# Heads and norm on ScalarE or GpSimd only, and another list of seeds for the order of a transformer block

## The chip, the cores and the metric

The kernel runs on one core of a Trainium2 chip. The metric is the time of one execution on the device in microseconds; the time before is the median of three runs, 952.11 us (951.52 to 952.36). The profile comes from one more execution, recorded by the hardware profiler. In it, TensorE multiplies matrices (PE; its weight loads are shown as PEld), VectorE (DVE), ScalarE (ACT) and GpSimd (POOL) do the element-wise work, and SyncE (SP) issues nearly all transfers. Each engine works through its own instructions strictly in order; semaphores hold an instruction back until what it needs is done.

## What is computed

A post-norm transformer block in float32: attention with grouped heads, then a gated feed-forward layer, each followed by a residual sum and a layer norm. There are 2 batches of 512 tokens, a model width of 512, 32 query heads and 8 key and value heads of width 128, and an inner width of 1376. Cut to what matters here:

```python
q = (x @ Wq.T).reshape(b, s, H, HD).transpose(0, 2, 1, 3)
k = (x @ Wk.T).reshape(b, s, HKV, HD).transpose(0, 2, 1, 3)
v = (x @ Wv.T).reshape(b, s, HKV, HD).transpose(0, 2, 1, 3)
q = _rmsnorm(q, q_norm_w)      # t * rsqrt(mean(t*t) + EPS) * w, over each head
k = _rmsnorm(k, k_norm_w)
scores = jnp.einsum('bkgqd,bksd->bkgqs', qg, k) / math.sqrt(HD)
bias = jnp.where(rel > 0, NEG_INF, slopes[:, :, None, None] * rel)
attn = jax.nn.softmax(scores + bias[None], axis=-1)
out = jnp.einsum('bkgqs,bksd->bkgqd', attn, v)
# ... out @ Wo.T, x = layernorm(x + attention), x = layernorm(x + ffn)
```

The part that the change names is `_rmsnorm`: the heads times their norm.

## The kernel before

**Tiles and stages.** The tokens of a batch are cut into four blocks of 128. A *unit* is (group g, batch b, block i): 8 groups of four query heads with one key and value head, 2 batches, 4 blocks, 64 units. Two neighbouring units make a *pair*, and there are 32 pairs. For each pair, `project` forms q, k and v of two blocks (with seven half-size products in place of eight: `seven`, L747; only the first pair is projected plainly, L867), `heads` normalises and transposes them, `scores` forms the scores and the softmax of each unit, `attend` multiplies with v, and `project_out` or `project_pair` multiply with Wo. After the attention come the layer norm (`norm1`), the feed-forward products (`ffn_up`, `ffn_down`) and the last layer norm.

**The heads and their norm** (`heads`, from L988). For each of the two blocks r of a pair, ScalarE squares 5 heads of 128 columns (four of q, one of k, L1002), VectorE reduces them to `ms` (L1025), GpSimd takes the power -1/2 (`rsqrt`, L674) into `inv`, and then `normed` multiplies the heads by `inv` into `sq`. This last step can be done in two ways: as one product of 128x640 with a broadcast operand on VectorE or GpSimd (L1072), or as five scaled copies of 128x128 on ScalarE (L1065). There are 64 such steps. From `sq`, VectorE transposes into `c` (L1188), which goes through `far_q` in DRAM (L1201) back into `qT` (L1212), and k is weighted into `kT` (L1226, L1228). The first pair goes over TensorE transposes instead (L1145, L1160).

**Scores and attention.** A score matmul (L1263) writes `sc`, VectorE adds the bias and takes the row maximum (L1272), ScalarE takes the exponential (L1288), VectorE the reciprocal of the row sums (L1303), ScalarE or GpSimd scale the rows (L1320, L1322). VectorE transposes squares of 32 into `st` (L968), SyncE stores `st` to `far` in DRAM (L977) and loads it back turned as `prT` (L1385), two loads for each block, and TensorE multiplies it with v (`pa`, L1408). Units 0, 1 and 63 are turned on TensorE instead (`pt`, L1359).

**Transfers.** All on SyncE's queue but for the first loads of xT and the last store, which stand on ScalarE's. Beside `far`, `prT`, `far_q` and `qT` these are the loads of weights: `w` of a group in chunks of 384 KB (L486), `wo` in one load of 1 MB (L541).

**What sets the order.** Every operation is first recorded as an op (`Work.add`): the engines that may do it with an estimated cost for each, a priority, and what it reads and writes. `emit` then plans and issues. `order` is a list scheduler: it keeps the free times of the engines and, step by step, takes the ready op that could start first; among ops of one engine that could start at the same time, the one of lowest `prio` wins. If an op may run on several engines, the engine is chosen there too. The order so found becomes the fixed order of each engine's instructions. Before that, `shift` is called once for every number in `SHIFTS` (L79): it takes the number as a random seed, draws a place in the range of priorities and a reach, and adds random amounts to the priorities of the ops there. The priorities of the plan are thus those written in the code plus the sum of all these shifts.

For the heads, the choice of engine is written so:

```python
NORMED = {"DVE": dve(5 * HD) + 0.2, "POOL": pool_tt(5 * HD), "ACT": 5 * act(HD, True)}
WHO = ("DVE", "POOL", "ACT")
...
W.add({k: NORMED[k] for k in WHO}, prio, normed, ...)
```

Of the kernel before, what the change touches and what calls it, by code (L numbers as in the profile page):

```python
# [60 lines left out]
def act(n, scaled=False):  # L61
    return 0.15 + 0.00084 * n + (0.1 if scaled else 0.0)


def dve(n):
    return 0.15 + 0.00106 * n


def pool_tt(n):
    return 0.27 + 0.00197 * n  # L70


def pool_ts(n):
# [3 lines left out]
LAG = {"PE": 0.22, "DVE": 0.1, "ACT": 0.12, "POOL": 0.2, "SP": 0.1, "ACTQ": 0.1, "NONE": 0.0}  # L77
TABLE = 1.28
SHIFTS = (  # L79
    42000001, 42000003, 42000019, 42000038, 42000046, 42000048, 42000080, 42000095, 42000168,  # L80
    42000176, 42000217, 42000257, 42000262, 42000308, 42000360, 42000448, 42000460, 42000471,
    42000478, 42000488, 42000493, 42000503, 42000508, 42000510, 42000517, 42000520, 42000530,
    42000532, 42000548, 42000582, 42000707, 42000844, 42000865, 42000884, 42000922, 42000957,
    42000970, 42000975, 42001005, 42001037, 42001049, 42001090, 42001148, 42001238, 42001283,
    42001404, 42001444, 42001471, 42001476, 42001778, 42002042, 42002048, 42002090, 42002122,
    42002149, 42002330, 42002340, 42002665, 42002784, 42002821, 42003002, 42003036, 42003133,
    42003139, 42003188, 42003348, 42003694, 42003791, 42004290, 42004466, 42005040, 42005857,
    42006497, 42006735, 42006892, 42007003, 42007117, 42007158, 42007651, 42008481, 42008514,
    42009150, 42011723, 42012356, 42012546, 42013135, 42013648, 42014108, 42014321, 42014614,
    42014976, 42015318, 42015996, 42016788, 42016932, 42017026, 42017104, 42017164, 42020579,  # L90
    42020641, 42021783, 42021971, 42022454, 42022740, 42023193, 42023363, 42024350, 42024865,
    42025415, 42026349,
)
NORMED = {"DVE": dve(5 * HD) + 0.2, "POOL": pool_tt(5 * HD), "ACT": 5 * act(HD, True)}
WHO = ("DVE", "POOL", "ACT")
ALONE = lambda p, r: False


# [255 lines left out]
def post_ln_block(  # L354
# [631 lines left out]
    def heads(p, prio):  # L986
# [67 lines left out]
        for r in range(2):  # L1054


            def normed(e, r=r):
# [16 lines left out]
            W.add(  # L1074
                {k: NORMED[k] for k in WHO},
                prio,
# [1167 lines left out]
```

## Time and profile before

| | |
|---|---|
| runs, median of 3 (lowest, highest) | 952.11 us (951.52, 952.36) |
| the profiled execution, its own time | 954.71 us |
| of it the span, first to last instruction | 952.9 us |
| granted TensorE clock, mean | 0.997 |
| transferred in the span | 157.46 MB, 165 GB/s |
| scores (L1263) on TensorE | 154.1 us in 512 records |
| projections (L747, all forms of `_q`) on TensorE, first form | 90.3 us in 248 records |
| power -1/2 (L674) on GpSimd, mean | 1966 ns |
| heads times norm on ScalarE (L1065) | 165 copies, mean 397 ns |
| landing of a prT load, median | 3.2 us |

How to read it: the profiled execution is one execution, and a little longer than the runs without a profile, so a sum over its instructions is compared with its own time. A float32 matmul gives two records in the trace, so 4254 records of TensorE stand for fewer instructions. Matmuls are pipelined: a record of 486 ns for 384 columns overlaps the next, and what counts is the distance from start to start, 1.29 us for four of them. The 40 slices of the span show TensorE at 9 tenths or more in all but the first and the last, and a granted clock of 9 tenths or more throughout. An idle time of TensorE is shown with what ended it; a wait of another engine costs nothing as long as TensorE doesn't wait in turn.

### The profile page before, as it was taken

The page shows a single profiled execution, that of the slowest core. Times are in us where ns is not written, and L with a number is a line of the kernel's source. Part 1 is how long each engine was busy: PE and PEld are TensorE (multiplying, and loading weights), DVE is VectorE, ACT ScalarE, POOL GpSimd, SP SyncE. Part 2 cuts the span into 40 slices and gives each one's busy share as a digit, 9 for nine tenths or more (in the row PEclk, how much of TensorE's full clock was granted, in tenths as well). Part 3 has the DMA queues.
Part 4 walks back from the last instruction along what each step waited for, and adds up shares of the span by engine and source line. Part 5 has one row for each costly group of instructions (what it writes and reads, how often), then busy time and mean ns, then how long its engine had stood idle before and what let it go on. Part 6 is the DMA issues. An engine that isn't in the chain of part 4 may idle for free.

```text
span 952.9 us, 14098 instructions
## 1 busy us (share of the span) xinstructions
PE 940.2 (99%) x4254; PEld 682.6 (72%) x4254; DVE 713.3 (75%) x1767; ACT 485.2 (51%) x1347; POOL 549.3 (58%) x608
## 2 busy tenths in 40 slices
PE   8999999999999999999999999999999999999997
PEld 5655776766767675767677766676677888888886
DVE  7777877778877878887878888787776766675464
ACT  3676665656565656465746566565652433433100
POOL 5774775657494837775768686866564412232040
PEclk9999999999999999999999999999999999999999
DMA  9269758555583847657678786569852323310011
GB/s 324 67 199 258 232 157 241 170 184 174 176 234 107 267 132 222 206 186 198 172 239 225 235 214 190 174 184 263 217 176 81 86 81 89 85 52 23 1 45 44
DMA packets 196876, 157.46 MB, mean 165 GB/s; under 512 B 28384, under 2 KB 179680, under 8 KB 195520
## 3 DMA queue, kind: packets, MB, share of 16 engines
q1 hardware_dynamic: 195936, 155.90, 54.8%
q8 instruction: 34, 0.56, 0.2%
q10 hardware_dynamic: 864, 0.66, 0.2%
q14 instruction: 42, 0.34, 0.1%
HBM read 97.60 MB, written 58.46 MB: 164 GB/s over the span
## 4 chain that ended last, share of the span: by engine, by line
PE 96%; DMA 2%; SPq 1%; DVE 0%; issue 0%; POOLq 0%; DVEq 0%
PE pa_q L747 17%; PE sc L1263 13%; PE pa L1408 12%; PE pb_q L747 8%; PE pa_h L747 8%; PE pa_o L1632 8%; PE pb_h L747 4%; PE pc_q L747 4%; PE pb_o L1632 4%; PE pa_d L747 4%; PE pa_o L747 3%; PE pc_o L1632 2%; PE pc_h L747 2%; PE pb_d L747 2%; PE px L1440 2%; DMA prT<-far 2%
## 5 line engine op out<-in xcount | busy, mean ns | idle before, releaser
L1288 ACT ACTIVATE pr<-pr,nmax 128x48 f32<-128x48 f32 (+15 forms) x256 | 133.4, 522 | 91.2 <-DVE nmax L1272 90.1
L1263 PE MATMUL sc<-kT,qT 128*128 128x512 f32 (+15 forms) x512 | 154.1, 409 | 0.0
L1272 DVE CUSTOM_DVE_ANT_0 pr<-sc,bias 128x48 f32<-128x48 f32 (+15 forms) x256 | 109.7, 442 | 34.3 <-PE sc L1263 31.5
L1408 PE MATMUL pa<-prT,v 128*128 128x512 f32 (+1 forms) x306 | 129.6, 512 | 2.7 <-DMA prT<-far 2.7
L1263 PEld LDWEIGHTS sc<-kT,qT 128*128 128x128 f32 x512 | 88.2, 191 | 48.2 <-issue 21.9
L1320 ACT ACTIVATE pr<-pr,rden 128x64 f32<-128x64 f32 (+12 forms) x221 | 95.4, 495 | 23.1 <-DVE rden L1303 22.8
L688 DVE TENSOR_TENSOR acc<-acc,pa_o 128x512 f32<-128x512 f32 (+2 forms) x128 | 72.7, 568 | 44.9 <-PE pa_o L1632 28.2
L968 DVE STREAM_TRANSPOSE st<-pr 128x512 f32<-128x512 f32 (+1 forms) x153 | 92.1, 634 | 1.6 <-ACT pr L1320 0.6
L747 PE MATMUL pa_q<-tq,sx 128*128 128x384 f32 x248 | 90.3, 487 | 0.0
L1408 PEld LDWEIGHTS pa<-prT,v 128*128 128x128 f32 x306 | 54.0, 191 | 24.3 <-issue 6.4
L674 POOL TENSOR_TENSOR inv<-ms,nhalf 128x10 f32<-128x10 f32 (+1 forms) x33 | 64.9, 1966 | 7.8 <-DVE ms L1039 5.4
L848 ACT COPY gu<-pa_h 128x256 f32<-128x256 f32 (+1 forms) x88 | 31.8, 370 | 73.3 <-PE pa_h L747 62.7
L1002 ACT ACTIVATE sq<-c 128x640 f32<-128x640 f32 x64 | 45.7, 730 | 38.3 <-DVE c L1188 32.9
L747 PEld LDWEIGHTS pa_q<-tq,sx 128*128 128x128 f32 x248 | 45.5, 190 | 26.9 <-issue 5.5
L848 ACT COPY c<-pa_q 128x384 f32<-128x384 f32 x73 | 34.5, 473 | 54.2 <-PE pa_q L747 47.4
L1065 ACT ACTIVATE sq<-c,inv 128x128 f32<-128x128 f32 x165 | 51.9, 397 | 15.0 <-POOL inv L674 15.0
L1188 DVE STREAM_TRANSPOSE c<-sq 128x320 f32<-128x320 f32 x124 | 55.8, 485 | 0.0
L1025 DVE TENSOR_REDUCE ms<-sq 128x5 f32<-128x640 f32 x64 | 51.4, 810 | 1.2 <-ACT sq L1002 1.2
L1632 PEld LDWEIGHTS pa_o<-ti,si 128*128 128x128 f32 x336 | 43.1, 192 | 7.2 <-issue 3.6
L688 POOL TENSOR_TENSOR so<-aT,aT 128x512 f32<-128x512 f32 x23 | 29.3, 1274 | 32.8 <-PE pa_o L1632 31.7
L1322 POOL TENSOR_SCALAR pr<-pr,rden 128x64 f32<-128x64 f32 (+7 forms) x67 | 31.1, 473 | 29.4 <-DVE rden L1303 28.3
L1288 ACT ACTIVATION_READ_ACCUMULATOR pr<-pr,nmax 128x1 f32 x256 | 48.0, 188 | 0.0
(245 smaller groups left out, 2216.9 us busy)
## 6 DMA issues: line engine op xcount, KB each, us to landing
far<-st SPq DMA_DIRECT2D x122, 256.0 KB, 3.1
prT<-far SPq DMA_DIRECT2D x244, 128.0 KB, 3.2
far_q<-c SPq DMA_DIRECT2D x31, 640.0 KB, 3.9
qT<-far_q SPq DMA_DIRECT2D x62, 320.0 KB, 3.8
w<-in_wqkv_dram SPq DMA_DIRECT2D x39, 384.0 KB, 4.6
wo<-in_wot_dram SPq DMA_DIRECT2D x10, 1024.0 KB, 5.8
far<-st SPq DMA_DIRECT2D x31, 128.0 KB, 2.7
prT<-far SPq DMA_DIRECT2D x62, 64.0 KB, 3.0
```

The costliest lines, as they stand in the source:

```text
L674: lambda e: nc.gpsimd.tensor_tensor(dst(), src(), nhalf[:, :n], ALU.pow),
L688: lambda e: vec[e].tensor_tensor(dst(), a(), b(), alu),
L747: nc.tensor.matmul(bank[:rows, :width], lhsT=a(fa, c), rhs=b(fb, c), start=(fresh and c == 0), stop=(c == depth - 1), skip_group_check=True,)
L848: nc.scalar.copy(dst(), src())
L968: {"DVE": dve(n)}, prio, lambda e: nc.vector.transpose(dst(), src()), reads, [A(st)]
L1188: lambda e, r=r, m=m: nc.vector.transpose(cb[:, m] .rearrange("p n w -> p (n w)")[:, :half] .rearrange("p (m r h d) -> p r h m d", m=2, r= ...
L1263: lambda e, a=a, w=w, sc=sc: nc.tensor.matmul(sc[:, :w], lhsT=qT[:, r, a, : G * Q], rhs=kT[:, :w], start=True, stop=True),
L1272: lambda e, a=a, w=w, sc=sc: nc.vector.tensor_tensor_reduce(out=pr[:, a, :w], in0=sc[:, :w], in1=bias[:, S - w :], scale=-(SHRINK**-g), sc ...
L1288: lambda e, a=a, w=w: nc.scalar.activation(pr[:, a, :w], pr[:, a, :w], AF.Exp, bias=nmax[:, a : a + 1], scale=-1.0, accum_out=den[:, a : a ...
L1320: nc.scalar.activation(dst, src, AF.Copy, scale=rden[:, a : a + 1])
L1408: lambda e, j=j, prT=prT, n=n: nc.tensor.matmul(by_head(po.tile)[:, :, P - n // G :], lhsT=v[:, j, :], rhs=late(prT, j, n), start=(j == 0) ...
L1632: nc.tensor.matmul(bank[:, ts(c, P)], lhsT=a(fa, c), rhs=b(fb, c), start=fresh and c == 0, stop=True, skip_group_check=True,)
```

## The change

It does two things. `WHO` no longer names VectorE, so that the planner can give the product of heads and norm to GpSimd or ScalarE alone. And the list of 110 seeds is replaced by another of 102, sought among 72000 numbers; not one is kept. Both go into the planner, which orders all ops anew: the operations, their sizes and their costs are the same, but for the engine of those that may run on several. The diff, cut in the middle of the two lists:

```diff
 TABLE = 1.28
 SHIFTS = (
-    42000001, 42000003, 42000019, 42000038, 42000046, 42000048, 42000080, 42000095, 42000168,
...
-    42025415, 42026349,
+    122000003, 122000005, 122000008, 122000019, 122000028, 122000065, 122000089, 122000102,
...
+    122065376, 122065661, 122065761, 122066904, 122067471, 122071425,
 )
 NORMED = {"DVE": dve(5 * HD) + 0.2, "POOL": pool_tt(5 * HD), "ACT": 5 * act(HD, True)}
-WHO = ("DVE", "POOL", "ACT")
+WHO = ("POOL", "ACT")
 ALONE = lambda p, r: False
```

## The prediction

> **What bounds the kernel now.** I read the busy shares first, then the chain of waits, then TensorE's own waits, because an engine at 99% can still hide slack.
>
> ```profile
> PE 940.2 (99%) x4254; PEld 682.6 (72%) x4254; DVE 713.3 (75%) x1767; ACT 485.2 (51%) x1347; POOL 549.3 (58%) x608
> ...
> PE 96%; DMA 2%; SPq 1%; DVE 0%; issue 0%; POOLq 0%; DVEq 0%
> ```
>
> TensorE is the bound: busy 940.2 of 952.9 us, and 96% of the chain that ended last. VectorE is in the chain with 0%, so an instruction taken from it is worth nothing by itself. What can be gained is what TensorE waits for, by the view of waits with TensorE alone:
>
> ```profile
> PE pa L1408 <- DMA prT<-far: 2.7, 2, 2.1
> PE pp L867 <- DMA w<-in_wqkv_dram: 1.8, 1, 1.8
> PE warm L554 <- POOL ident masks.py:199: 1.3, 1, 1.3
> PE pb_q L747 <- DVE ms L1039: 0.5, 1, 0.5
> PE pp L867 <- DMA xT<-in_xt_dram: 0.4, 1, 0.4
> ```
>
> Where they lie is in the timeline of TensorE. The first is the wait at the head, the next two lie around 688 us:
>
> ```profile
> 9.87 7.98 PE L867 MATMUL pp<-w,xT 128*128 128x384 f32 x24 [1.77 <-DMA w<-in_wqkv_dram]
> ```
>
> ```profile
> 685.65 0.33 PE L1263 MATMUL sc<-kT,qT 128*128 128x64 f32 x2
> 688.09 2.05 PE L1408 MATMUL pa<-prT,v 128*128 128x512 f32 x2 [2.11 <-DMA prT<-far]
> 689.92 0.61 PE L1263 MATMUL sc<-kT,qT 128*128 128x112 f32 x2
> 690.33 1.58 PE L747 MATMUL pa_o<-to,so 128*128 128x256 f32 x4
> 691.75 1.02 PE L1408 MATMUL pa<-prT,v 128*128 128x512 f32 x2
> ```
>
> The stall costs more than its 2.11 us. A pair of 128x512 products takes 0.86 us from start to start elsewhere in the chain; here it takes 689.92 - 688.09 = 1.83. The pair of 112 columns takes 0.41 where it takes 0.22, the four of 256 take 1.42 where they take 0.86, and the start is 2.22 late: 2.22 + 0.97 + 0.19 + 0.56 = 3.9 us. The table by stretches (columns: sum of the stretch, busy time of the five engines, granted clock, DMA share, GB/s) says why:
>
> ```profile
> 688.00:690.00 2.00, 1.92 (x3) 0.92 (x4) 0.00 (x0) 0.74 (x3) 0.37 (x1) 0.50 0.98 321
> 690.00:692.00 2.00, 2.00 (x8) 1.71 (x7) 0.34 (x3) 0.48 (x2) 0.00 (x0) 0.65 0.20 68
> ```
>
> The granted clock is 0.50 and 0.65 there. **Rule against row:** the Trainium skill, "TensorE: Matmul & The Clock Gate" (What's actually happening), has the array fall to half rate after an idle window of about 3.4 us. The idle row here is 2.11 us and the clock fell all the same, so the measurement decides: a stall of this size is priced at 3.9 us; by the rule it would be 2.2.
>
> **What the change does, part by part.** The work is the same: the built orders of both kernels hold 2170 TensorE and 682 SyncE instructions. What moves is the order, on every engine.
>
> *The norm's engine.* Of the 64 products of heads and norm, 7 stood on VectorE, 24 on GpSimd, 33 on ScalarE; now it is 0, 31, 33. The rows by line:
>
> ```profile
> L1072 POOL TENSOR_TENSOR sq<-c,inv x24: 1250/1256/1346, 49.4 to 666.1; 128x640 f32<-128x640 f32 x24
> ...
> L1072 DVE TENSOR_TENSOR sq<-c,inv x7: 817/820/2434, 38.9 to 523.5; 128x640 f32<-128x640 f32 x7
> ```
>
> VectorE gives up 7 x 1.10 = 7.7 us (mean 1101 ns), GpSimd takes 7 x 1.26 = 8.8. The skill speaks against this: "GPSIMD Engine Reference" (Engine selection) sends elementwise work to VectorE and calls GpSimd about twice as slow for two inputs. By that rule each move costs its chain some 1.1 us, by the medians 0.44, by the means, with the one 2434 ns instruction, 0.16. I take 0.44. It lies beside other work: from a pair's last product to its first score matmul the new order leaves at least 20.2 us of TensorE work (22.7 before). The chain between them by rows: 0.56 sum, 0.74 squares, 0.81 reduce, 0.2, 1.98 power, 1.26 norm, 4 x 0.45 transposes, 3.9 landing, 0.55 issue, 3.8 landing, 0.4 weighting = 16.0. That covers 0.44 nine times, so the move costs 0; without the cover, 7 x 0.44 = 3.1. Nor is VectorE relieved: counted by kind, with mean durations from the rows, other two-input sums move to it, and its total goes up by 4.8 us, GpSimd's goes down by 14.5, ScalarE's by 4.4. All stay under TensorE.
>
> *The head.* The chain from the start runs through SyncE's issues of qw and kw (0.43 us each), then the last chunk of w, issued at 5.47 and landed at 9.73. The new order issues that chunk before qw and kw: 0.95 us earlier (5.47 - 4.52), so about 8.8. More: TensorE now takes the chunks of w in the order in which they are issued, so ten products, not four, stand ahead of the first that needs the last chunk. The first four end at 5.04 + 3.06 = 8.10; six more of 0.645 us put the demand at 11.97. The wait of 1.77 us goes: -0.95 at least, -1.77 taken. Late next is the second half of xT of batch 1: it lands up to 9.5 us after an issue at 8.51, at 18.0, and is wanted at 8.10 + 7.74 + 3 x 1.29 = 19.7. I take 0, up to +1.
>
> *At 20.93* TensorE waits 0.51 us behind VectorE's sum on xT; the new order has that sum on GpSimd, several instructions ahead. -0.5 (ends 0 and -0.7).
>
> *At about 40 us* the second unit gets tight: 0.43 us of TensorE work between its last transposes and the product that reads their eviction, where an eviction of 128x512 by ScalarE takes 0.59. With hand-overs: +0.4 (0 to 1).
>
> *The two stalls on prT.* Both waits (648.10, 0.61 us idle and slower after it, 0.8 in all; and 688.09) are for loads of prT that SyncE issues right behind a 1 MB load of wo: 7.5 and 7.0 us in the chain, where the page's median to landing is 3.2. As a measure I take the TensorE work, from rows, between the last TensorE event that the load's issue depends on through deps, buffers and queue order, and the matmul that reads it. Behind a load of wo this lead was 8.6 at the first stall and 9.8 at the second; 7.9 and 10.5 to 10.9 at others that did not stall. At the same two loads of wo the new order has 23.6 and 11.3. I take both stalls as gone: -0.8 and -3.9 (ends: both stay, 0); late next there is the next block of prT, with over 10.
>
> *What comes instead.* The trace cannot show the new order, so bounds. A plain chain to prT costs by rows 0.44 (scores on VectorE) + 0.63 (transposes) + 0.36 (issue of far) + 2 x 0.57 (issues of prT) + 3.2 (landing) = 5.8 us. The new order's tightest leads of several steps are 5.6 (with four issues of prT: 2.3 + 3.2 = 5.5), 6.9, 7.3, 7.4, 7.6 and 7.7 (with three transposes: 7.0); before they were 6.6, 7.0, 7.1, 7.3. Behind loads of wo it has 7.9 and 8.3, behind loads of w 7.5 and 7.9, where 7.7 did not stall before. So nothing must stall, and more places can. Below: 0. Above: two stalls like that at 688, 7.8. I take 2.5, nearest to one short stall and its slow clock.
>
> **Sum**, against the profiled execution (954.71 us, of it span 952.9): -1.8 - 0.5 + 0.4 - 0.8 - 3.9 + 2.5 = -4.1, so 950.6. That execution lies 2.6 above the median of the runs, 952.11; the same difference gives **948.0**.
>
> **Rivals.** *Slower: stalls behind weights.* One mechanism: SyncE's queue is in order, and a load of w waits there for TensorE to release its buffer; the prT loads queue behind it and share the DMA engines with it. Places: w of group 3 ahead of the first unit of group 1 (lead 7.5), wo of groups 1 and 3 (8.3, 7.9), w of group 6 (7.9). For it: in both stalls before, landing took over 7 us. Against: leads of 7.7 and 7.9 held. Each costs 3.9 us; without new stalls the sum is -6.6, so two bring +1.2, and it decides from the third: 952.1 - 6.6 + 11.7 = 957.2. *Same: the gain is eaten.* One stall like that at 688, and only 0.95 won at the head: -5.8 + 3.9 = -1.9, 950.2, and with xT late, 951.5. *The words only:* engine shares move, TensorE's waits don't: 952.1, since no VectorE time is on the chain. Against it: the head's issue order is different in the built program.
>
> **Numbers.** A measurement of this kernel tells 0.2% or 1.9 us from no change. Forecast, 948.0 (944.8 to 950.2): 0.73. Gain eaten, 951.5: 0.12. Words only, 952.1: 0.04. Slower, 957.2 (and milder, from 954.0): 0.11. Faster 0.73, same 0.16, slower 0.11. The range goes from 944.8 (no new stall, -6.6, and the ends of the small terms) to 952.8, which takes in both middle cases and leaves the slow one out.
>
> **What would show it.** Right: the second batch of pp starts near 8.1, not 9.87; no wait of TensorE on prT near 648 and 688; clock 1.00 in all stretches between; VectorE busy near 718, GpSimd near 535. Wrong: waits of TensorE on prT of over 2 us, with a load of w or wo issued just ahead; or a wait on xT at 20 us that gives the head back.

## The result, and the profile after

The change makes the kernel slower: 957.48 us, median of 4 runs (956.76 to 957.96), beside 952.24 (951.52 to 953.07) for the kernel before. The ratio is 1.0051 with a 95% interval of 1.0039 to 1.0064; the forecast was 948.0 with a range to 952.8. In the experiments below the kernel before was run again with each set, 951.3 to 956.1 with medians of 952.7 to 953.2.

The page of after, busy times and the chain that ended last:

```profile
span 956.2 us, 14134 instructions
...
PE 941.0 (98%) x4254; PEld 681.6 (71%) x4254; DVE 715.5 (75%) x1782; ACT 481.4 (50%) x1336; POOL 536.9 (56%) x604
...
PE 92%; DMA 5%; DVE 1%; SPq 1%; ACT 0%; issue 0%; POOL 0%; POOLq 0%; DVEq 0%; ACTq 0%
```

TensorE is still the bound, and its own work is the same. Its share of the chain is down from 96% to 92%, and DMA is up from 2% to 5%: what was added is waiting. The view of TensorE's waits (total us, times, longest us):

```profile
PE pa L1408 <- DMA prT<-far: 5.4, 6, 1.4
PE pb_q L747 <- POOL xT L688: 1.7, 1, 1.7
PE warm L554 <- POOL ident masks.py:199: 1.3, 1, 1.3
```

The head did what was forecast: all 32 records of `pp` stand in one row of the timeline, without a wait, and `pa_q` follows at 15.72, where it stood at 17.68 before.

```profile
4.38 11.50 PE L867 MATMUL pp<-w,xT 128*128 128x384 f32 x32
15.72 1.45 PE L747 MATMUL pa_q<-w,xT 128*128 128x384 f32 x4
```

The waits at 20.93, 648 and 688 are gone too. In their place, the timeline of TensorE in after:

```profile
45.48 1.56 PE L747 MATMUL pb_q<-w,xT 128*128 128x384 f32 x4 [1.72 <-POOL xT L688]
...
690.53 1.13 PE L1408 MATMUL pa<-prT,v 128*128 128x512 f32 x2 [1.18 <-DMA prT<-far]
...
694.04 1.10 PE L1408 MATMUL pa<-prT,v 128*128 128x512 f32 x2 [1.09 <-DMA prT<-far]
...
702.72 1.10 PE L1408 MATMUL pa<-prT,v 128*128 128x512 f32 x2 [0.70 <-DMA prT<-far]
...
711.97 1.10 PE L1408 MATMUL pa<-prT,v 128*128 128x512 f32 x2 [1.41 <-DMA prT<-far]
```

One long stall has become many short ones: one near 45 us, four within 22 us at the end of the attention, and three of 0.3 to 0.55 at 81.7, 460.6 and 555.3, which other executions of this order of TensorE have in part or not at all.

To see where the time went, I subtract TensorE's own work from its clock. Each product is counted at its undisturbed distance from start to start (1.29 us for four records of 384 columns, others in proportion; a record of fewer than 128 columns counts as 128, and a group of the `px` and `pz` products as the 1.08 that it takes); the sum up to a given product is its position. Time of the trace less position is what TensorE has lost by then. The marks are the groups of `px` products (L1440), sixteen in each kernel, of which the first, the thirteenth and the last are taken. All values in us, of one profiled execution each:

| kernel | lost up to the first mark | first to thirteenth | thirteenth to last | sum |
|---|---|---|---|---|
| before | 7.2 | 7.3 | 6.1 | 20.7 |
| after | 7.9 | 8.9 | 7.1 | 23.9 |

(Before: marks at 88.99, 624.79, 731.19, positions 81.8, 610.2, 710.5. After: 86.61, 623.18, 736.93, positions 78.7, 606.4, 713.1.) The difference of 3.2 is nearly all of the 3.3 between the spans. The head's gain of 2 is used up by the first mark, 1.6 is lost in the middle, and the last stretch, whose two stalls went, loses 1.0 more than before. The 1.6 is the least firm of these: among the executions below, the middle loses 7.3 to 8.0 in the order of before and 7.4 to 9.8 in the order of after, though none of their moves but that of the norms lies in it. By kind, the 3.2 are 3.9 more at the starts that a wait delayed (9.6 against 5.7 over their undisturbed distance), 1.4 less of slow clock (0.5 against 1.9, 1.7 of it behind the stall at 688), and 0.7 in the small rest. The runs differ by 5.2, not 3.3; why is taken up with the second group of experiments.

### The profile page after: what moved, and what is told of

Its sections match the earlier page's. It is cut to its first block, busy times and chain, and to the rows that moved or that the text cites. A ratio compares the mean times of both kernels' runs of the same rounds, so it can differ in the third digit from the quotient of the medians.

```text
span 956.2 us, 14134 instructions
## 1 busy us (share of the span) xinstructions
PE 941.0 (98%) x4254; PEld 681.6 (71%) x4254; DVE 715.5 (75%) x1782; ACT 481.4 (50%) x1336; POOL 536.9 (56%) x604
## 4 chain that ended last, share of the span: by engine, by line
PE 92%; DMA 5%; DVE 1%; SPq 1%; ACT 0%; issue 0%; POOL 0%; POOLq 0%; DVEq 0%; ACTq 0%
PE pa_q L747 16%; PE sc L1263 12%; PE pa L1408 10%; PE pa_h L747 8%; PE pa_o L1632 8%; PE pb_q L747 8%; PE pb_h L747 4%; PE pb_o L1632 4%; PE pc_q L747 4%; PE pa_d L747 4%; DMA prT<-far 2%; PE pa_o L747 2%; DMA qT<-far_q 2%; PE pc_o L1632 2%; PE pc_h L747 2%; PE pb_d L747 2%
## 5 line engine op out<-in xcount | busy, mean ns | idle before, releaser
L1263 PE MATMUL sc<-kT,qT 128*128 128x240 f32 (+15 forms) x512 | 152.8, 408 | 0.6 <-ACT kT L1226 0.3
L1320 ACT ACTIVATE pr<-pr,rden 128x64 f32<-128x64 f32 (+12 forms) x210 | 90.6, 495 | 18.8 <-DVE rden L1303 18.6
L848 ACT COPY c<-pa_q 128x384 f32<-128x384 f32 x80 | 37.8, 474 | 76.6 <-PE pa_q L747 72.3
L1322 POOL TENSOR_SCALAR pr<-pr,rden 128x64 f32<-128x64 f32 (+12 forms) x78 | 37.1, 485 | 50.0 <-DVE rden L1303 49.6
L747 PE MATMUL pb_q<-w,xT 128*128 128x384 f32 x124 | 45.5, 489 | 1.7 <-POOL xT L688 1.7
```

Source lines behind the costliest of these rows:

```text
L747: nc.tensor.matmul(bank[:rows, :width], lhsT=a(fa, c), rhs=b(fb, c), start=(fresh and c == 0), stop=(c == depth - 1), skip_group_check=True,)
L848: nc.scalar.copy(dst(), src())
L1263: lambda e, a=a, w=w, sc=sc: nc.tensor.matmul(sc[:, :w], lhsT=qT[:, r, a, : G * Q], rhs=kT[:, :w], start=True, stop=True),
L1320: nc.scalar.activation(dst, src, AF.Copy, scale=rden[:, a : a + 1])
```

## Experiments

Four kernels change the engine or the plan; the others leave the plan as it is and move single ops in the finished order, with a helper put into `emit` (`move(ns, to)` puts the ops with these numbers, one by one, ahead of op `to`). TensorE's order is untouched by these moves, so the marks can be compared between kernels. The inserted lines shift the line numbers in their profiles by 4 to 11.

```diff
-        for o in self.order():
+        placed = self.order()
+        def move(ns, to):
+            for n in ns:
+                o = next(x for x in placed if x["n"] == n)
+                placed.remove(o)
+                placed.insert(next(i for i, x in enumerate(placed) if x["n"] == to), o)
+        ...
+        for o in placed:
```

| kernel | median, us | ratio to before | 95% interval |
|---|---|---|---|
| after | 957.48 | 1.0051 | 1.0039 to 1.0064 |
| norm_to_gpsimd | 952.78 | 0.9996 | 0.9987 to 1.0005 |
| norm_to_vectore | 959.02 | 1.0063 | 1.0051 to 1.0076 |
| engines_alone | 969.39 | 1.0169 | 1.0152 to 1.0185 |
| seeds_alone | 981.51 | 1.0303 | 1.0288 to 1.0318 |
| before_head | 951.78 | 0.9988 | 0.9980 to 0.9996 |
| before_wo | 950.59 | 0.9977 | 0.9965 to 0.9989 |
| before_both | 949.90 | 0.9973 | 0.9962 to 0.9983 |
| before_three | 950.08 | 0.9966 | 0.9953 to 0.9978 |
| xT_first | 956.72 | 1.0036 | 1.0024 to 1.0049 |
| vn_later | 954.52 | 1.0009 | 1.0001 to 1.0018 |
| wo_later | 958.10 | 1.0055 | 1.0040 to 1.0070 |
| three_moves | 959.49 | 1.0064 | 1.0052 to 1.0076 |
| after_mended | 959.92 | 1.0078 | 1.0065 to 1.0092 |
| after_two | 954.20 | 1.0014 | 1.0007 to 1.0020 |
| after_four | 954.68 | 1.0017 | 1.0010 to 1.0025 |

### Is it the engine?

**norm_to_gpsimd**: the order of before, and only the engine of seven ops changed.

```diff
+        for o in placed:
+            if o["fn"].__name__ == "normed" and o["eng"] == "DVE":
+                o["eng"] = "POOL"
```

> The order of before, kept as it is, with only the 7 products of heads and norm that stood on VectorE given to GpSimd. Theory (the order costs the time, not the engine): no change, 952.2, at most +1. Rival (the engine costs it: each of the 7 norms is later and its pair's scores with it): +3 to +5, 955 to 957.

**norm_to_vectore**: the order of after, and the same seven pairs back on VectorE (`c_1`, `c_8`, `c_10`, `c_13`, `c_16`, `c_21`, `c_24`).

> The order of after, kept as it is, with the products of heads and norm of the same 7 pairs given from GpSimd to VectorE. Theory (order): no change against after, 957.5, within 1. Rival (engine): 3 to 5 less, 953 to 954.5.

Moving the seven norms to GpSimd costs nothing: 0.9996, with both ends within 0.13%. Its profile has all of them on GpSimd (this view gives the shortest, median and longest duration in ns), VectorE 6.5 us less busy and GpSimd 9.1 more than before:

```profile
L1076 POOL TENSOR_TENSOR sq<-c,inv x31: 1255/1257/1481, 38.4 to 665.8; 128x640 f32<-128x640 f32 x31
```

```profile
PE 939.0 (99%) x4254; PEld 681.4 (72%) x4254; DVE 706.8 (74%) x1760; ACT 484.9 (51%) x1347; POOL 558.4 (59%) x615
```

The way back gains nothing either (1.0063 beside 1.0051, the intervals overlap). The rival is out: the engine of the norm, by itself, is not where the 5 us come from.

**engines_alone** and **seeds_alone**: one half of the diff each, planned anew.

> The kernel before with WHO of two engines and the old seeds, planned anew. Theory (order): a third order with waits of its own; its time can be on either side, 948 to 960, and its distance from before equals the difference of TensorE's waits and slow rows. If it is slower than before while the first kernel of this set is not, the planner's order and not the engine did it. Rival (engine): 955 to 957, with waits of TensorE on kT or qT behind the power and the norm.

> The kernel after with WHO of three engines again, and the new seeds, planned anew. Theory (order): a fourth order, 948 to 960; sums over TensorE's waits explain it. Rival (engine): the time of before or less, 952 or below, since VectorE may take norms again.

Both missed the range given: 969.39 and 981.51. Each half alone is far worse than both together, so the effects of engine list and seeds don't add. In seeds_alone one wait for VectorE is of 5.8 us, the longest in any of these kernels:

```profile
PE sc L1263 <- DVE nmax L1272: 6.0, 2, 5.8
```

Neither list of seeds did well with the other choice of engines, and a small difference in the plan's input gave an order with other waits. Before and after are both orders with few waits, and what tells them apart is a handful of places.

### What were the gains worth?

**before_head** takes over the head's order of loads in part, **before_wo** moves the two loads of `wo` that stood ahead of the stalled loads of `prT`, **before_both** does both.

```diff
+        move([7], 11)            # before_head, before_both: chunk of w
+        move([3361], 3554)       # before_wo, before_both: wo of group 7, batch 0
+        move([3643], 4023)       # before_wo, before_both: wo of group 6, batch 1
```

> Before, with one load moved on SyncE: the chunk of w that TensorE wants for its fifth product goes ahead of two chunks that it wants later, and of qw and kw. Theory (the head's gain of the new order is this load's place): the wait of 1.77 at 9.87 goes, -1.8 against before, 950.9. Rival (the start is bound by what lands behind it, xT or the other chunks): no change, 952.8.

> Before, with two loads of wo (1 MB) moved on SyncE: that of group 7, batch 0, behind the two prT loads that it delayed at 648, that of group 6, batch 1, behind the four that it delayed at 688. Theory (as the prediction had it, both stalls are loads of prT behind a load of wo and go with it): -4.7 against before, 948. Rival (the 1 MB takes its time on the DMA engines wherever it stands, and the next loads of prT, with leads no longer, stall in their place): -1 to +2, 952 to 955.

> Before, with the moves of both. Theory: their sum, -6.5, 946.3. Rival: -1.8 to 0, 951 to 953.

Every gain has the sign foreseen, and every one is smaller: 1.2 per mille at the head (1.1 us) instead of 1.8 us, 2.3 per mille for the two stalls (2.2 us) instead of 4.7, and 2.7 per mille (2.6 us) for both. The two waits on `prT` are gone. TensorE's waits in before_both, but for its first:

```profile
PE pb_q L757 <- DVE ms L1049: 0.5, 1, 0.5
PE pp L877 <- DMA xT<-in_xt_dram: 0.3, 1, 0.3
PE sc L1273 <- POOL kT L1238: 0.2, 1, 0.2
```

Why less than the trace of before promised? before_head and norm_to_gpsimd leave the two stalls where they were, and show them in two more executions. From the thirteenth mark to the last it took 106.4 us in before, 104.2 in before_head, 104.7 in norm_to_gpsimd, and 101.9 in before_wo. So the stalls cost 4.5 us in the profiled execution of before and 2.3 and 2.8 in the others. The same stall in before_head, and the stretches of it (columns as in the prediction's table):

```profile
686.09 1.10 PE L1416 MATMUL pa<-prT,v 128*128 128x512 f32 x2 [1.61 <-DMA prT<-far]
```

```profile
686.00:688.00 2.00, 1.91 (x8) 1.28 (x8) 0.28 (x2) 0.71 (x4) 0.38 (x1) 1.00 1.06 333
688.00:690.00 2.00, 2.00 (x10) 1.30 (x9) 1.35 (x6) 1.36 (x6) 0.88 (x2) 1.00 0.22 76
```

The idle time is 1.61 in place of 2.11, and the clock stays at 1.00. The profiled execution of before had a slow clock behind its stall: 2.2 us more from the thirteenth mark to the last than before_head. That fits most of the 2.6 us by which it exceeded the median of the runs, and most of the difference between the 3.3 of the spans and the 5.2 of the runs.

The wait at the head isn't worth its length either. before_wo has the head of before, and there the same product starts at 9.80 after a wait of 0.82, where before's started at 9.87 after 1.77: the products ahead of it ended at 8.98 there and at 8.10 in before (full clock from 6.4 and from 5.3 us), and the wait took up the difference.

**before_three** also moves the sum on xT that TensorE waited for at 20.93 ahead of a reduction on VectorE (`move([156], 75)`).

> As before_both, with one move on VectorE: the sum on xT of the first batch goes ahead of a reduction of 0.81 that it stood behind. Theory (as the prediction had it): the wait of 0.51 near 19.5 goes, -0.5 against before_both, 949.4. Rival (the reduction is then late, and the first unit's scores with it): +0.3 to +1, 950.2 to 951.

The wait shrank from 0.51 to 0.31 in its trace. The view of before names `ms`, which ended just then; the move shows that it was the sum on xT that TensorE waited for. 950.08 beside 949.90, with ratios of 0.9966 and 0.9973: a gain of this size can't be told here. before_both and before_three are faster than both kernels of the case.

### Where do the new waits come from?

**xT_first** (`move([405], 105)`): in after, GpSimd's queue had the sum on xT behind a sum that waits for VectorE. The timeline of GpSimd in after:

```profile
43.48 1.26 POOL L688 TENSOR_TENSOR ti<-wo,ti 128x512 f32<-128x512 f32 x1 [1.60 <-DVE ti L688]
44.71 0.72 POOL L688 TENSOR_TENSOR xT<-xT 128x256 f32<-128x256 f32 x1
```

> After, with one move on GpSimd: the second batch's sum on xT goes ahead of a sum on wo that waits for VectorE (the wait of 1.7 us of TensorE at 45.48). Theory (it waits only for its place in GpSimd's queue): the wait goes, -1.5 against after, 956.0. Rival (another wait takes its place a product later): no change, 957.5.

The wait on xT is gone, and the next product waits in its place, for the sum on sx, which VectorE makes behind two reductions of 0.8:

```profile
46.25 1.56 PE L755 MATMUL pa_q<-tq,sx 128*128 128x384 f32 x4 [1.48 <-DVE sx L696]
```

By the first mark it was 1.3 us ahead of after, of which 0.3 was there before the move. The medians differ by 0.8, and the intervals overlap.

**vn_later** moves the four copies of v for the last pair (`move([4009, 4010, 4011, 4012], 3977)`). The queue of SyncE in after, ahead of the stall at 694.04, with one issue right behind the other:

```profile
686.68 1.28 SPq L1385 DMA_DIRECT2D prT<-far  x2
688.01 0.63 SPq L1097 DMA_DIRECT2D vn<-c  x1
688.74 0.56 SPq L1201 DMA_DIRECT2D far_q<-c  x1
689.40 1.74 SPq L1385 DMA_DIRECT2D prT<-far  x2
```

The loads issued at 689.4 are those that TensorE waits for until 694.04, although the store that they read, issued at 684.74, had landed at 687.05.

> After, with one move on SyncE: the four copies of v for the last pair (vn<-c of pair 31, 0.63 to 0.7 us of issue each) go behind the loads of prT that they stood ahead of, between 684 and 700 us. Theory (SyncE's queue, full of issues back to back, brings these loads late): the waits of TensorE at 690.5 (1.18), 694.0 (1.09) and 702.7 (0.70) go or shrink, -2 to -3.5 against after, 954 to 955.5. Rival (the stores' and loads' own landing, or the DMA engines, set it): 0 to -0.8, 956.7 to 957.5.

The largest effect of the moves in after: 954.52, 1.0009 in place of 1.0051, some 3 to 4 us. No wait is left at the products that stood at 690.53 and 694.04; here they are in vn_later, with 0.38 at the product that waited 0.70:

```profile
690.30 1.10 PE L1416 MATMUL pa<-prT,v 128*128 128x512 f32 x2
...
698.88 1.10 PE L1416 MATMUL pa<-prT,v 128*128 128x512 f32 x2 [0.38 <-DMA prT<-far]
```

From the thirteenth mark to the last it took 111.8 us where after took 113.8, so the traces place 2.0 us of the gain there; the rest isn't placed, since the stretches ahead differ by as much between executions of one order. In after, the three loads that ended these waits landed 3.1, 3.9 and 3.4 us after their issue, where the median is 3.1: they were late mainly by their turn in SyncE's queue. No weights stand there.

**wo_later** moves the last load of wo behind two loads of prT (`move([3889], 3954)`).

> After, with one move on SyncE: the last load of wo (1 MB, issued at 703.3) goes behind the two loads of prT that it stood ahead of. Theory (the loads landed in 5.7 to 6.0 us behind the 1 MB): they land in about 3.2, the wait at 711.97 (1.4) goes, -1.4 against after, 956.1. Rival (the load is late for another reason, or later loads take the delay): no change, 957.5.

Here the rival is right. The wait at 711.97 went, and two longer ones came behind it:

```profile
716.21 0.67 PE L1416 MATMUL pa<-prT,v 128*128 128x256 f32 x2 [2.37 <-DMA prT<-far]
718.76 1.19 PE L1416 MATMUL pa<-prT,v 128*128 128x256 f32 x2 [1.88 <-DMA prT<-far]
```

SyncE's queue shows why. The stores of far and two small copies to vs now stand right behind the 1 MB:

```profile
705.12 0.54 SPq L549 DMA_DIRECT2D wo<-in_wot_dram  x1
705.75 0.90 SPq L985 DMA_DIRECT2D far<-st  x2
706.78 1.83 SPq L1116 DMA_DIRECT2D vs<-c  x2
713.07 3.48 SPq L1393 DMA_DIRECT2D prT<-far  x4
```

The next loads of prT read what these stores write, and are issued at 713.07 only. The vs copies landed 8.6 and 7.6 us after their issue, the stores of far 7.3 and 9.1 (2.4 and 2.9 are the medians of their sizes). The loads themselves then took 2.3 to 2.7.

**three_moves** does these three together.

> After, with the three moves together. Theory (nine microseconds of small waits of the new order make its time, each with its own place in a queue): the sum of the three, -5 to -6.5 against after, 951 to 952.5. Rival (the stretch around 700 is bound by its DMA traffic, and a wait removed comes back behind it): at most -2, 955.5 or more.

The moves don't add up: 959.49, slower than after. With the earlier waits gone the same stores stand behind wo, TensorE waits for 2.94 us near 715, and the clock goes to 0.50.

**after_mended** was to repair that: wo and the vs copies behind all those loads (`move([3889, 4013, 4014], 4172)`), and the sums on xT and sx forward. In it a sum on sx reads xT ahead of the sum that makes it, so part of q, k and v of the second batch comes out wrong; the amount of work is the same, and its time is shown for the waits alone.

> After, with the copies of v moved as before, the last load of wo and the two vs copies moved behind all loads of prT of the last three units, and the sums on xT and sx of the second batch moved forward on GpSimd and VectorE. Theory (each small wait has its place in a queue and can be mended there, if what follows is looked at): against after, -3.5 for the copies of v, -1.4 for wo, -1.5 for the sums: 951. Rival (TensorE's lead is too short in this stretch for any order of the loads): 954 to 958.

959.92. Now it is the next load of weights that stands behind wo: `wi`, of the feed-forward layer. (The sum on xT wasn't mended either: it waits for a sum on sx, and TensorE for it, 2.16 us at 45.06.) ScalarE converts `wi`, and has to evict a block of prT of the last unit next (first row ScalarE, second TensorE):

```profile
718.63 1.37 ACT L859 CAST wf<-wi 128x512 f32<-128x512 int32 x2 [7.23 <-DMA wi<-in_gwt_dram]
```

```profile
720.54 1.27 PE L1419 MATMUL pa<-prT,vn 128*128 128x512 f32 x2 [2.88 <-ACT prT L859]
```

**after_two** makes the moves of vn_later and moves the sums in their right order (`move([405, 406, 407], 334)`); **after_four** also puts vs behind the loads of prT (`move([4013, 4014], 4168)`) and wo behind the first two loads of wi (`move([3889], 4197)`).

> After, with the copies of v moved as before, and the sum on xT and the two sums on sx that need it moved forward together, each behind the one it reads, on GpSimd and VectorE. Theory (small waits of the new order, each with its place in a queue, add up): -4.0 for the copies and -1.5 for the sums, 952.0. Rival (beyond the copies of v the time has another cause): 953.5 to 955, no less than with the copies alone.

> As after_two, and on SyncE the two copies to vs go behind the loads of prT of the last units, and the last load of wo behind those and behind the first two loads of wi, which ScalarE converts ahead of an eviction that TensorE waits for. Theory (the 1 MB of wo costs whatever is issued right behind it, and little where nothing behind it is wanted soon): the waits near 707.8 and 713.7 go and none of 2.9 near 720 comes, -1.5 against after_two, 950.5. Rival (the load of wo is itself wanted by then, or what remains is bound by the chain of the last units): no gain, 952 or more.

Neither beats the copies alone: 954.20 and 954.68 beside 954.52. In after_two TensorE no longer waits 1.7 near 45, but the reductions that were passed make the power late, and GpSimd weights kT behind it:

```profile
45.30 1.56 PE L756 MATMUL pa_q<-tq,sx 128*128 128x384 f32 x4 [0.33 <-DVE sx L697]
...
51.85 1.32 PE L1272 MATMUL sc<-kT,qT 128*128 128x304 f32 x4 [1.12 <-POOL kT L1237]
```

In after_four the waits at 707.8 and 713.7 are gone, and one on ScalarE's eviction, again behind the conversion of wi, takes their place:

```profile
717.32 1.12 PE L1419 MATMUL pa<-prT,vn 128*128 128x512 f32 x2 [2.14 <-ACT prT L859]
```

The losses by the same marks as above, for the kernels with TensorE's order of after, and before_both beside them:

| kernel | up to the first mark | first to thirteenth | thirteenth to last | sum |
|---|---|---|---|---|
| after | 7.9 | 8.9 | 7.1 | 23.9 |
| vn_later | 7.8 | 7.7 | 5.1 | 20.6 |
| wo_later | 8.0 | 8.0 | 10.9 | 26.9 |
| after_two | 7.2 | 7.3 | 5.4 | 19.9 |
| after_four | 7.5 | 8.3 | 5.3 | 21.0 |
| before_both | 6.3 | 7.5 | 1.7 | 15.6 |

Each figure is of one profiled execution. From the thirteenth mark to the last no order of the loads tried here brings after below 5.1, where the old order of the products, with its loads of wo moved, loses 1.7. What part of these 3.4 us lies in TensorE's order itself and what in other queues, the runs don't tell apart.

## Why the prediction was wrong

**What bounds the kernel, and where the gains were**: right. TensorE's waits were the place to look, and all four that were to go went. The head came 2.0 us earlier, with nothing behind it on xT; the waits at 20.93, 648 and 688 are absent.

**The engine of the norm at 0**: right, shown by norm_to_gpsimd. GpSimd was as slow as the row said (1257 ns), and the 0 fits the cover of over 20 us that was assumed; the cover itself was not varied. VectorE was less busy than forecast (715.5, near 718 said), GpSimd as forecast (536.9, near 535).

**"As a measure... I take both stalls as gone: -0.8 and -3.9"**: the mechanism is right, the size is not. Both terms came from one execution, in which the clock had dropped behind the stall. In the runs the two stalls are worth 2.2 us (before_wo), not 4.7. The price of 3.9 for a stall of this size held in that execution and not in the others, by how much idle time fell into one window of the clock (2.02 us there, 1.61 and 1.70 in before_head and norm_to_gpsimd; last section). The 2.6 us by which that execution exceeded the median was carried over as a constant; by the 2.2 above it was in large part the slow clock itself, which I had subtracted already. The head, 1.8 in the sum, brought 1.1 in before_head, which takes over only part of the new order there.

**"What comes instead. ... I take 2.5"**: this is the step that failed. In the profiled executions the sum needed a span of 952.9 - 4.1 = 948.8, and the span is 956.2: with the other terms as they stood, this one should have been 9.9, beyond its upper end of 7.8. Its bound was wrong in kind: it counted long stalls, two at most, by the leads of the loads of prT. What came were ten waits, none over 1.72 us and together 8.0, where before's five behind the first were together 5.4. The cluster at 690 to 703 was made in good part by turns in SyncE's queue, with issues of 0.6 us each back to back, where I had looked at the leads alone: moving the four copies of v out of these turns took 3 to 4 us from the runs (vn_later), the larger part of the 5.2. And the wait at 45.48 is on no load at all: I had looked at the head and the second unit, but not the sums on xT of the second batch, behind GpSimd's wait for VectorE. With the copies and the sums both mended (after_two) the kernel is still 1.0014 of before; the cause of this rest stays open.

**The rivals**: the slower one named 957.2, and the runs gave 957.5, but that is luck: the reason was another. Its mechanism, stalls of 3.9 us behind weights at groups 1, 3 and 6, didn't happen; of the waits that came, only that at 711.97 stands behind a load of weights (its loads took 5.7 to 6.0 us), and it is of 1.4. "The words only" is refuted for the order, and confirmed for the engine.

**The signs named beforehand**: "right" was tied to the absence of waits at known places, and these signs all appeared; "wrong" was tied to waits of over 2 us. Neither spoke of the sum of waits, which is what decided.

## What to carry to other kernels

When a whole order is replaced, the gains can be listed from the old trace and the losses can't; two orders that were each sought for the fewest waits differ in the places, and a sum that has all of one side and a guess for the other leans towards a gain. Count the turns in a queue as well as the leads: at each place where several loads are wanted within a few microseconds, add up the issues ahead of them. And a wait is worth what the next wait leaves of it: the moves in the better order paid (before_head, before_wo and before_both), while in the worse one each move but that of the copies met the next late thing, sx behind xT, kT behind sx, a store or wi behind wo.

## What the runs showed of the hardware

**The clock after an idle time.** From its first rise on, the trace lists the stretches of time in which the granted clock stayed the same. In all 17 profiled executions, each of them but the last, which the end cuts off, is a whole multiple of 3.41 us: in before 682.67 us at full clock, which is 200 such windows, then one window at half. So the clock is set anew once in 3.41 us, and by the traces what counts is how long TensorE was idle within one such window. Ahead of 935 us, seven windows at full clock held 1.92 us of idle time or more (1.92 to 3.31), and behind each the clock was 0.50 for one to three windows, 3.4 to 10.2 us. Of those with 1.80 or less, only one was followed by the half clock, with 1.16 (engines_alone, ending at 637.1); why, the runs don't show. Behind the last products windows with up to 1.99 kept the full clock, so the border is not sharper than 1.9 to 2.0.

This tells stalls of nearly the same length apart. Of the 2.11 in before, 2.02 fell into one window; the 2.14 in after_four was cut by a border, with 0.68 idle in one window and 1.45 in the next. Here are these windows and, for before, the one behind (columns as in the stretches above; idle is the first number less TensorE's):

```profile
684.59:688.00 3.41, 1.39 (x8) 1.06 (x6) 2.36 (x10) 1.12 (x6) 0.77 (x2) 1.00 1.20 213
688.00:691.42 3.42, 3.33 (x7) 2.15 (x8) 0.28 (x2) 1.22 (x5) 0.37 (x1) 0.50 0.68 224
```

```profile
712.45:715.86 3.41, 2.73 (x17) 2.12 (x16) 1.27 (x3) 0.62 (x1) 0.97 (x1) 1.00 0.86 253
715.86:719.28 3.42, 1.96 (x8) 1.19 (x9) 2.29 (x5) 1.95 (x4) 0.96 (x1) 1.00 0.79 286
```

So a stall of some 2 us has two prices, with and without the slow clock: 1.9 us in before_head (1.61 idle) and 3.9 in before. The Trainium skill names an idle window of about 3.4 us for the half rate ("TensorE: Matmul & The Clock Gate", What's actually happening); the windows of the traces have that length, but 1.92 us of idle time in one were enough.

**A load of 1 MB delays what is issued right behind it, loads, stores and copies alike.** In after, loads of prT behind it took 5.7 to 6.0 us where 3.1 is the median; in vn_later the same loads took 4.0 to 4.2. In wo_later a store of far took 7.3 where 2.4 is the median, and the two copies to vs took 8.6 and 7.6.
